# Two graph layers on one core: weight bursts of seven pairs, a seventh pair in the spare accumulator bank, and two numerators moved

## The chip, the cores and the metric

The kernel runs on one core of a Trainium2 chip. The metric is the device time of one execution in microseconds (us). The engines are named as in the profile: PE is TensorE's matmul, PEld its weight load, DVE is VectorE, ACT is ScalarE, POOL is GpSimd, SP is SyncE, which here only issues transfers. All data are float32, some of it in the reduced form float32r[...].

## The reference

There are B = 8 batches, N = 2048 nodes and C = 64 features. `A` is the row-normalised adjacency matrix. Both layers add a graph convolution to x and normalise:

```python
def layer0(x, A, embedding, weight, bias):        # K = 3
    As = [I, A, 2 * A @ A - I]
    w = einsum('nd,dkio->nkio', embedding, weight)      # a weight matrix for each node
    x_g = einsum('knm,bmc->bnkc', stack(As), x)
    return einsum('bnki,nkio->bno', x_g, w) + embedding @ bias

def layer1(x, E, A, weights_pool, bias_pool):
    supports = [I, A, 2 * A @ A - I, softmax(relu(E @ E.T), axis=1)]
    # the same three einsums with four supports

x = layernorm(x + layer0(x, adj, ...))
x = layernorm(x + layer1(x, E, adj, ...))
```

The node embeddings have D = 16 elements. Three kinds of work follow from this: products of an adjacency block with x or with `u = A x` (called *products* here), the making of the *weights* w of each node from its embedding, and the *apply*, which multiplies each node's features by its own weights.

## The kernel before

**Stages.** The nodes are cut into 8 blocks of 256. There are five phases of 8 stages, one per block j: A0 (stages 0 to 7, u = A x of layer 0), B0 (8 to 15, A u), A1 (16 to 23), Z1 (24 to 31, the softmax support) and V1 (32 to 39). Most stages form their product by Strassen's scheme: seven products p1 .. p7 in the order `usual = (1, 4, 7, 2, 6, 5, 3)` (other orders for the first and the last stage of V1). Each product has 8 steps, so such a stage has a length of 56 steps. DVE and ACT read a product's accumulator when it is done and combine the parts: p1 and p4 are copied by ACT, the others are added by DVE.

**The plan.** Everything that isn't a product is written into a plan by hand: `put(n, place, job)` puts a job into stage n at a place between 0 and 64, which is scaled to the stage's length (place x 56/64 steps). While PE goes through the products of stage n, each job is issued after the first step that reaches its place. All instructions are pinned, so on every engine the order of the program is the order of execution[...].

**Weights.** `Stage.weights` (L327) makes w for the 256 nodes of a block. A *pair* here is two matmuls of 64 rows each (h = 0 and h = 1), one on the upper and one on the lower half of TensorE's rows[...]. Their stationary operand is a part of a chunk `wst` (8 pairs; 512 KB, loaded by SP), the moving one is `e2`, the block's embeddings. Two pairs fill one buffer `pw`: two PSUM banks, one for each half. Then ACT or DVE copies the buffer into `w_room`, the only room for w. A full stage has 32 pairs in 16 groups of two. They are made in bursts of three groups (`cuts = (0, 3, 6, 9, 12, 14, 16)`), since the pool `ps_big` has three buffers of two banks. They go round in turn among all users: `pw`, the apply's `po`, the turn's `pt`, scores `ps`, row scores `pr`, bias `pb`. V1 begins with one group alone at place 4. The stages of A0, B0 and A1 have their weights made in the following stage, those of V1 in their own.

**Accumulators.** The other two banks are `ps_acc`, one bank each, used in turn by the products: while one is filled, the other is read.

**Other jobs that the text speaks of.** `apply` (L348) fills four `po` buffers, one after the other, and DVE takes each in by four SCALAR_TENSOR_TENSOR. In V1 the four applies of the previous stage stand at place 4, ahead of the weights at the same place. `turn` (L414) transposes u or x through a buffer `pt`; half of it is copied to `t` by ACT, half by DVE. In A1 the turn of u stands at place 4 of the next stage. `statistics` (L722) runs two exponentials on ACT, at place 62 of an A1 stage (for j = 0 at 19 of the next). `Sums.make` (L746) forms the right-hand sums of Strassen's scheme on DVE. `numerators` (L676) makes exponentials of scores for the softmax support; in stage 24 they serve stage 25, which is called narrow, at places 3, 5, 7 and 10, with two `normalize` at 37 and 40.

**Weight loads.** `Ahead` (L228) keeps up to three chunks: `next` first fills, that is it issues the load of the next chunk into the room that came free, and then hands out the oldest.

## Time and profile before

| what | value |
|---|---|
| time, median of 3 runs (lowest to highest) | 1467.65 us (1466.69 to 1468.63) |
| the profiled execution | 1470.19 us, of which the span is 1468.3 us |
| granted TensorE clock | 0.998 |
| PE MATMUL of the weights, pw | 1728, 297 ns each by the profile, 146.5 us busy |
| ACT copies w <- pw, 128x1024 | 330, 1021 ns each |
| DVE copies w <- pw, 128x1024 | 118, 1224 ns each |
| DVE evacuation of the applies, acc <- po | 640, 426 ns each |
| DMA wst <- wd, 512 KB, SP | 108, 6.1 us from issue to landing |

Durations of matmuls overlap[...]. So the cost of a stretch of PE's work is read from the starts, by taking the distance from the first start to the start of what follows.

In the timeline each line has the start, the time until the last of its instructions ends, the engine, the source line (all have L43, since a helper issues them), the operation, the tiles written and read, the shape and the count; in brackets the idle time before and what ended it. In the list of waits a line has who waited, what for, the total in us, how many times, and the longest.

### The profile page before, as it was taken

Reading aid. Unit: us, or ns where it says so; the run is one execution under the profiler, and the core shown is the slowest. Engines: PE = TensorE matmul, PEld = TensorE weight load, DVE = VectorE, ACT = ScalarE, POOL = GpSimd, SP = SyncE. Lnnn points to the kernel's source line nnn. Section 1 sums busy time; section 2 is a strip of 40 time slices with the busy share of each in tenths; the row PEclk is TensorE's granted clock in tenths of the full one; section 3 lists DMA queues with packets and bytes.
Section 4 is the critical chain, followed back from the end, with each engine's and each line's share of the span. In section 5 each row is a group of like instructions: output and inputs, shape, how many; then the busy total and the mean of one; then the engine's idle time right before and its main releaser. Section 6 shows DMA issues by size and latency. Waiting matters only on the chain.

```text
span 1468.3 us, 31599 instructions
## 1 busy us (share of the span) xinstructions
PE 1440.8 (98%) x13502; PEld 1184.9 (81%) x13502; DVE 973.9 (66%) x1655; ACT 478.3 (33%) x597; POOL 204.6 (14%) x339
## 2 busy tenths in 40 slices
PE   9999999999999999999999999999999999999996
PEld 4577777778999999567777777799888988888885
DVE  3866666648676766865666666679794666666666
ACT  0444444432211213154444344612110233333332
POOL 4212221110111111211011111011000000000000
PEclk9999999999999999999999999999999999999999
DMA  9888888886666666578887977223313766666662
GB/s 361 274 262 276 282 280 265 281 313 190 209 192 201 205 201 206 157 177 180 205 201 162 207 205 186 35 73 101 90 44 105 236 196 190 189 194 191 190 206 59
DMA packets 88380, 285.50 MB, mean 194 GB/s; under 512 B 14000, under 2 KB 19632, under 8 KB 86640
## 3 DMA queue, kind: packets, MB, share of 16 engines
q1 hardware_dynamic: 55568, 175.13, 41.0%
q0 software_dynamic: 27200, 94.71, 21.4%
q10 hardware_dynamic: 5472, 13.63, 2.8%
q8 instruction: 107, 1.75, 0.5%
q14 instruction: 33, 0.27, 0.1%
HBM read 217.33 MB, written 62.41 MB: 191 GB/s over the span
## 4 chain that ended last, share of the span: by engine, by line
PE 91%; DVE 4%; DMA 3%; ACT 1%; issue 1%; ACTq 0%; DVEq 0%
PE p L43 58%; PE po L43 14%; PE pw L43 9%; PE pu L43 4%; PE pz L43 4%; DMA wst<-wd 2%; PE pt L43 1%; PE pr L43 1%; PE ps L43 1%; DVE acc L43 1%; DMA x<-in_x 1%; DVE u L43 1%; DVE t L43 0%; DVE p L43 0%; ACT t L43 0%
## 5 line engine op out<-in xcount | busy, mean ns | idle before, releaser
L43 ACT ACTIVATE w<-pw 128x1024 f32<-128x1024 f32 x330 | 320.1, 1021 | 444.4 <-PE pw L43 442.6
L43 DVE SCALAR_TENSOR_TENSOR acc<-po,mask,acc 128x256 f32<-128x256 f32 (+1 forms) x640 | 247.1, 426 | 66.8 <-PE po L43 56.5
L43 DVE COPY w<-pw 128x1024 f32<-128x1024 f32 x118 | 144.4, 1224 | 142.3 <-PE pw L43 142.1
L43 PE MATMUL p<-a,u 128*128 128x128 f32 x1920 | 234.1, 278 | 0.6 <-issue 0.6
L43 PEld LDWEIGHTS p<-a,u 128*128 128x128 f32 x1920 | 221.2, 192 | 8.8 <-issue 2.4
L43 PE MATMUL po<-w,t 128*32 128x256 f32 (+1 forms) x5120 | 206.9, 337 | 7.0 <-issue 5.8
L43 PE MATMUL p<-u,a 128*128 128x256 f32 x832 | 204.3, 388 | 0.0
L43 PEld LDWEIGHTS po<-w,t 128*32 128x32 f32 (+1 forms) x5120 | 128.3, 108 | 79.3 <-issue 16.3
L43 PEld LDWEIGHTS p<-u,a 128*128 128x128 f32 x832 | 151.6, 190 | 29.2 <-issue 5.4
L43 PE MATMUL p<-x,a 128*128 128x256 f32 x624 | 152.4, 384 | 0.0
L43 PE MATMUL pw<-e,wst 64*128 64x256 f32 x1728 | 146.5, 297 | 4.3 <-DMA wst<-wd 2.5
L43 PEld LDWEIGHTS pw<-e,wst 64*128 64x128 f32 x1728 | 112.5, 184 | 46.0 <-issue 23.9
L43 PEld LDWEIGHTS p<-x,a 128*128 128x128 f32 x624 | 114.7, 190 | 19.3 <-issue 0.5
L43 PE MATMUL p<-a,x 128*128 128x128 f32 x768 | 93.0, 277 | 0.0
L43 PEld LDWEIGHTS p<-a,x 128*128 128x128 f32 x768 | 88.3, 192 | 2.5 <-PE pw L43 0.2
L43 PE MATMUL pu<-x,a 128*128 128x512 f32 x192 | 87.0, 600 | 2.1 <-DMA x<-in_x 2.1
L43 PE MATMUL p<-w,u 128*128 128x256 f32 x384 | 85.8, 379 | 0.0
L43 PE MATMUL p<-a,w 128*128 128x128 f32 x672 | 81.3, 277 | 0.0
L43 PEld LDWEIGHTS p<-w,u 128*128 128x128 f32 x384 | 72.0, 190 | 9.3
L43 PEld LDWEIGHTS p<-a,w 128*128 128x128 f32 x672 | 77.3, 192 | 2.5 <-issue 1.4
L43 PEld LDWEIGHTS pu<-x,a 128*128 128x128 f32 x192 | 35.1, 190 | 42.7 <-issue 37.1
L43 DVE TENSOR_TENSOR temps<-p,temps 128x256 f32<-128x256 f32 x115 | 45.8, 420 | 34.1 <-PE p L43 33.3
(129 smaller groups left out, 1372.7 us busy)
## 6 DMA issues: line engine op xcount, KB each, us to landing
wst<-wd SPq DMA_DIRECT2D x108, 512.0 KB, 6.1
a<-in_adj_q SPq DMA_DIRECT2D x90, 512.0 KB, 5.3
a<-sd SPq DMA_DIRECT2D x88, 512.0 KB, 4.6
sd<-a POOLq DMA_DIRECT2D x24, 512.0 KB, 6.3
bx<-bx POOLq DMA_DIRECT2D x32, 256.0 KB, 5.9
acc<-bx POOLq DMA_DIRECT2D x16, 512.0 KB, 7.1
pd<-acc POOLq DMA_DIRECT2D x16, 512.0 KB, 5.3
acc<-pd POOLq DMA_DIRECT2D x16, 512.0 KB, 8.7
```

What stands on the lines that cost most here:

```text
L43: return self._tc.keep_in_program_order(f(*args, **kwargs))
```

## The change

The weights are now cut in pairs, not in groups. In 21 stages (the weights of A0 with j = 1 to 6, of A1 with j = 0 to 6, and of all of V1) the cuts are 0, 4, 11, 18, 25, 32: one burst of four pairs and four of seven. Six of the seven fill the three buffers of two banks; the seventh goes into the accumulator bank that no product is using. As that is one bank for both halves[...]: the h = 0 half is issued first in the burst and the h = 1 half last, the others are shifted by one against each other, and the last one waits for a read of one element by ACT from the first one's result. The other stages keep their bursts. The accumulator pool is written as two tags of one buffer, so that the spare one can be named. The copies are dealt anew: one group in each burst goes to DVE (with exceptions in A0 and V1), the single seventh pair is copied by ACT, second in order. Chunks are loaded at the end of a burst instead of at the start of the next. The places of the bursts change with their number, in A0 the turn, the apply and the post that follow move by 1 to 1.5 places, and the numerators of the narrow stage are set further apart.

```diff
-    ps_acc = ctx.enter_context(tc.tile_pool(name="ps_acc", bufs=2, space=PSUM))
+    ps_acc = ctx.enter_context(tc.tile_pool(name="ps_acc", bufs=1, space=PSUM))
...
+    in_use = [0]
+    in_turn = mybir.DependencyInfo(mybir.DependencyClass.Sync, mybir.DependencyReason.DATA)
+
+    def acc_bank(i):
+
+        return ps_acc.tile([P, BC], F32, tag=f"acc{in_use[0] ^ i}", name="pa")
...
-        def next(self):
-            self.fill()
+        def next(self, fill=True):
+            if fill or not self.ready:
+                self.fill()
             return self.ready.pop(0)
...
+        def weights(self, v0, v1):
+            if v0 == 0:
                 self.w = w_room[:, 0:NB * self.units].rearrange("p (n o) -> p n o", n=NB)
...
+                self.ws = {}
+            for c in range(v0 // 8, (v1 - 1) // 8 + 1):
+                if c not in self.ws:
+                    self.ws[c] = wst.next(fill=False)
+            pairs = list(range(v0, v1))
+            made = [(v, big("pw").rearrange("p h (v n) -> p h v n", n=NB)) for v in pairs[:-1:2]]
+            spare = []
+            if len(pairs) % 2:
+                spare = [pairs.pop()]
+                made.append((spare[0], acc_bank(1).rearrange("p (h v n) -> p h v n", h=2, n=NB)))
+            for at in zip(spare + pairs, pairs + spare):
+                for h, v in enumerate(at):
+                    r = slice(64 * h, 64 * h + 64)
+                    i, ps = (v - v0) % 2, made[(v - v0) // 2][1]
+                    ins = pe.matmul(ps[:, h, i, :], self.ws[v // 8][r, v % 8, :], self.e2[r, :], start=True, stop=True)
+
+                    if v in spare and not h:
+                        seen = act.activation(small.tile([1, 1], F32, tag="seen", name="seen"), ps[0:1, h, i, 0:1], AF.Copy)
+                    elif v in spare:
+                        tc.add_manual_dep(ins.ins, seen.ins.name, in_turn, reason="one bank, two row tiles")
+            wst.held = 1 if v1 % 8 else 0
+            wst.fill()
+            if spare:
+                made.insert(1, made.pop())
+            for k, (v, ps) in enumerate(made):
+                m = 1 if v in spare else 2
+                dst = self.w[:, :, 2 * v:2 * v + 2 * m].rearrange("p n (v h) -> p n v h", h=2)
+                on_dve = k == len(made) // 2 and v not in spare and self.n and (v > 16 if self.phase == "A0" else self.phase != "V1" or v0)
+                copy(0 if on_dve else 1, dst, ps.rearrange("p h v n -> p n v h"))
...
         def accumulator(self, name):
-            return ps_acc.tile([P, BC], F32, tag="acc", name=name)
+            in_use[0] ^= 1
+            return acc_bank(0)
...
-        cuts = (0, 3, 6, 9, 12, 14, 16) if st.units == C else (0, 3, 6, 8)
-        if phase == "V1" and st.j:
-            put(n, 4, st.weights, 0, 1)
-            cuts = (1, 4, 7, 10, 13, 16)
+
+        sevens = phase == "V1" or n in (*range(1, 7), *range(16, 23))
+        cuts = (0, 6, 12, 16) if st.half else (0, 4, 11, 18, 25, 32) if sevens else (0, 6, 12, 18, 24, 28, 32)
         weights = [(st.weights, *g) for g in zip(cuts, cuts[1:])]
+
+        def place_weights(n, places):
+            for place, job in zip(places, weights):
+                put(n, place, *job)
...
-            spread(n + 1, 1, 31, weights)
-            turned, bursts, posts = 33, (38, 38, 38, 38), (50,)
+            if sevens:
+                place_weights(n + 1, (1, 5, 14, 23, 32))
+                turned, bursts, posts = 34.5, (39.5, 39.5, 39.5, 39.5), (51,)
+            else:
+                spread(n + 1, 1, 31, weights)
+                turned, bursts, posts = 33, (38, 38, 38, 38), (50,)
...
-            spread(n + 1, 12, 34.5, weights)
+            if sevens:
+                place_weights(n + 1, (1, 6, 14, 23.2, 32.3))
+            else:
+                spread(n + 1, 12, 34.5, weights)
             turned, bursts, posts = 4, (43, 43, 43, 43), (56,)
...
-            spread(n, (22 if 0 < st.j < 7 else 12 if st.j else 4), (62 if st.j < 7 else 42), weights)
+            place_weights(n, (4, *((14, 23.2, 32.3, 41.5) if st.j in (0, 7) else (23.2, 32.3, 41.5, 50.7))))
...
-            for t, places in enumerate(((3, 5, 37), (7, 10, 40))):
+            for t, places in enumerate(((3, 7, 22), (37, 39.5, 57))):
```

More of the change, by code (lines that the diff above doesn't have):

```diff
@@ L324, in bias @@
                 pool.dma_start(out=rows, in_=heads(bx))
-        def weights(self, g0, g1):
-            if g0 == 0:
+        def weights(self, v0, v1):
+            if v0 == 0:
                 self.w = w_room[:, 0:NB * self.units].rearrange("p (n o) -> p n o", n=NB)
-            made = []
-            for g in range(g0, g1):
-                if g % 4 == 0:
-                    self.ws = wst.next()
-                ps = big("pw").rearrange("p h (v n) -> p h v n", n=NB)
-                for i in range(2):
-                    for h in range(2):
-                        r = slice(64 * h, 64 * h + 64)
-                        pe.matmul(ps[:, h, i, :], self.ws[r, 2 * (g % 4) + i, :], self.e2[r, :],
-                                  start=True, stop=True)
-                made.append(ps)
-            if g1 == self.units // 4:
-                wst.fill()
-            for g, ps in zip(range(g0, g1), made):
-                dst = self.w[:, :, 4 * g:4 * g + 4].rearrange("p n (v h) -> p n v h", h=2)
-                copy(0 if self.n and g % (8 if self.phase == "A0" else 3) == (2 if self.phase == "A0" else 1) else 1, dst, ps.rearrange("p h v n -> p n v h"))
+                self.ws = {}
[26 more added lines that the diff above has]
+                copy(0 if on_dve else 1, dst, ps.rearrange("p h v n -> p n v h"))
```

## The prediction

> **What bounds the kernel now.** I read the page first (busy shares, chain of waits, groups), then the timeline of TensorE (PE) in one V1 stage, then the same for VectorE (DVE) and ScalarE (ACT) at the two places where the change puts new work, then the list of waits of PE.

> ```profile
> PE 1440.8 (98%) x13502; PEld 1184.9 (81%) x13502; DVE 973.9 (66%) x1655; ACT 478.3 (33%) x597; POOL 204.6 (14%) x339
> ...
> PE 91%; DVE 4%; DMA 3%; ACT 1%; issue 1%; ACTq 0%; DVEq 0%
> ...
> L43 ACT ACTIVATE w<-pw 128x1024 f32<-128x1024 f32 x330 | 320.1, 1021 | 444.4 <-PE pw L43 442.6
> ```

> PE sets the end: it is busy 98% of the span and makes 91% of the chain. So every microsecond taken from PE's stream counts, and every wait put into it counts too. ACT is idle two thirds of the time, and its largest work is copying the weights.

> ```profile
> 1228.89 0.51 PE L43 MATMUL pw<-e,wst 64*128 64x256 f32 x4
> 1229.32 2.27 PE L43 MATMUL p<-a,u 128*128 128x128 f32 x18
> 1231.44 5.30 PE L43 MATMUL p<-a,x 128*128 128x128 f32 x46
> 1236.67 0.98 PE L43 MATMUL pw<-e,wst 64*128 64x256 f32 x12
> 1237.57 2.27 PE L43 MATMUL p<-a,x 128*128 128x128 f32 x18
> ```

> Starts count here (ends overlap). A burst of 2 pairs takes 0.43 us up to the next product matmul, one of 6 pairs 0.90: so (0.90 - 0.43)/4 = 0.118 per pair and 0.195 fixed. 46 product matmuls in 5.23 are 0.112 each, less the last, which stands 0.205 before the burst (0.093 too much); 18 right after a burst take 2.11 instead of 2.01. Each burst costs 0.195 + 0.093 + 0.10 = **0.39 to 0.40 us beside its pairs**.

> ```profile
> 1223.85 7.90 DVE L43 SCALAR_TENSOR_TENSOR acc<-po,mask,acc 128x256 f32<-128x256 f32 x16 [2.60 <-PE po L43]
> ```

> This is DVE evacuating the four po buffers that precede the burst at 1228.89: 0.494 us each, so the third buffer is free at 1223.85 + 12 x 0.494 = 1229.8, after that burst began.

> ```profile
> 753.23 1.15 ACT L43 ACTIVATE sq<-sq,low 128x1024 f32<-128x1024 f32 x1 [3.85 <-DVE low L43]
> ...
> 754.38 1.14 ACT L43 ACTIVATE row<-row,low 128x1024 f32<-128x1024 f32 x1
> 755.42 0.19 ACT L43 ACTIVATION_READ_ACCUMULATOR row<-row,low 128x1 f32 x1
> 755.63 1.26 ACT L43 ACTIVATE t<-pt 64x512 f32<-64x512 f32 x2
> ```
> ```profile
> 756.92 1.40 DVE L43 COPY t<-pt 64x512 f32<-64x512 f32 x2 [3.45 <-ACT t L43]
> ```

> This is the start of stage 20 (A1, j = 4; it begins at 752.53). ACT runs two exponentials until 755.61, then half of the turn's copies; DVE's half waits for ACT's and ends at 758.3. The burst at 758.24 takes that buffer last, and just gets it.

> ```profile
> PE pw L43 <- DMA wst<-wd: 2.5, 4, 0.8
> ...
> PE ps L43 <- DVE t L43: 1.3, 1, 1.3
> ...
> PE pw L43 <- DVE p L43: 0.7, 1, 0.7
> ```

> PE's few waits: late weight chunks in A1, and two waits in stage 24, where numerators crowd the turn.

> [...]The trace's plain copies agree in the slope (375 ns for 256 columns, 1021 for 1024: 0.84 ns), but leave 0.16 us for the fixed part.[...]

> **The change, part by part.** Own time of the profiled execution: 1470.19 us, its span 1468.3; the median is 1467.65, 2.5 less. I sum differences and add them to the median.

> 1. *Fewer bursts.* Twenty-one stages (weights of A0 j = 1..6, A1 j = 0..6, all of V1) go from six bursts to five with the same 32 pairs: 21 x 0.40 = **-8.4**.

> 2. *The small read*, 4 per such stage, 84 in all. The ordered product is the last of the burst; its weight load is due 0.224 + 5 x 0.113 - 0.11 = 0.68 us after the burst's start (intervals of single matmuls at 1236.67 and after). The first pair ends at 0.39 (389 ns is the longest pw matmul), ACT starts 0.08 after a pw group's end, the read takes 0.16 to 0.18, and PE resumes 0.05 after ACT's end (ACT's u ends at 626.94, PE's transposes start at 626.99): 0.69. So it is late by some 0.04. Bounds: nothing, if the read is quicker[...]. I take 0.04: 84 x 0.04 = **+3.4** (0 to 12.6). ACT stands free at nearly all bursts: in A0 with all copies on ACT (0.92 us apart for a big one, about 0.5 for the small one, then a 0.39 temps copy) it is done 4.3 us after a burst, and the next comes after 4.7. In stage 2 a DMA issue on ACT waits for the sums' store until 81.0: **+0.5** once. The spare's copy comes second and ends 2.2 to 2.3 us after the burst's start, the next product wants the bank after 2.5 to 2.7: covered.

> 3. *V1, first burst now four pairs.* The buffers go round by three: x, y, z, x for the four applies, then y, z for the burst's two groups. Before, only y was used. Now the second group needs z, the third apply's, free at 1229.8; its weight load is due at 1228.89 + 0.34 - 0.11 = 1229.12 and starts at 1229.84, and four pairs that took 0.67 (168.82 to 169.49) take 1.38. +0.71 in seven stages (j = 1..7): **+5.0**. ACT and DVE have time to spare at the other V1 bursts (p6's adds of 1.6 us fit in the 2.0 before the next burst).

> 4. *V1, j = 0.* The spare bank of the burst at place 23.2 is that of p2, whose adds stand in DVE behind three sums of 2.29 us and a weight copy: two sums from 1152.1 to 1159.0 (the old copy between them is gone), the copy to 1160.2, the third sum to 1162.4, the adds to 1163.2. The burst comes 20.5 steps of 0.446, one burst of four pairs and one of seven after 1150.49, at 1161.7: **+1.5**. The last burst moves from 62 to 41.5, and the po wait of 0.4 at 1183.7 goes: **-0.4**.

> 5. *A1, bursts at 1 and 6 around the turn at 4.* In stage 20's times: the first burst starts at 753.05 and delays the turn by 0.67 + 0.20 to 755.12..755.99; the next burst starts at 756.95. ACT: exponentials to 755.61, then the first group's copy (queued ahead of the turn's) to 756.64, the turn's two to 757.9; DVE's two follow, to 759.3. The seven-pair burst takes three buffers, and its third is the one of the transposes: due 757.4, free 759.37. **+2.0 us** in each of six stages (18 to 23; the exponentials lie alike in all six): +11.8. In stage 17 the exponentials are earlier but u's copy ends at 626.94: its burst waits 1.4, while the old 1.0 before the turn shrinks to 0.2: +0.5. Together **+12.3**.

> 6. *Weight loads.* The fill now follows the burst; in A1 chunk 3 is issued near 758 and wanted near 767.9, 9.9 us later; in the three stages with a real wait the load took 8.6 to 8.7 and was wanted some 0.8 sooner. The waits of 2.5 go: **-2.5**. SP's queue holds the adjacency loads behind each weight load as before.

> 7. *Numerators of stage 25 in stage 24.* At 3, 7 and 37, 39.5 they no longer claim the turn's buffer: the waits of 1.34 and 0.75 go, with some 0.2 of restarts: **-2.3**. The normalisations (2.3 us of DVE each) lie beside the products; first use is in stage 25.

> 8. Other bursts keep their sizes; who copies which group shifts by one or two, at no cost while PE has 2.8 us or more between them.

> Sum: -8.4 + 3.4 + 0.5 + 5.0 + 1.5 - 0.4 + 12.3 - 2.5 - 2.3 = **+9.1**. 1467.65 + 9.1 = 1476.8 (1479.3 for a profiled execution).

> **Rivals.**
> - *Faster: the A1 wait isn't there.* One mechanism: whether the turn's buffer is free when the seven-pair burst of A1 asks for it (part 5). If ACT serves the turn in time, 11.8 + 1.4 drop out: 9.1 - 13.2 = -4.1, **1463.5**. It decides from 0.6 us per stage instead of 2.0 (9.1 - 6 x 1.4 = 0.7). For it: the old burst got the same buffer without a wait. Against: it did so by some 0.2 us only (free at 758.31, its weight load due near 758.6), and both the earlier place and the extra ACT copy go the wrong way.
> - *The read is dear.* At 0.15 late each, 84 x 0.15 = 12.6 instead of 3.4: +18.3, **1486**. For it: it is in line 84 times[...]. Against: the 0.16 us from this trace.
> - *A balance.* The A1 wait half as long and the read hidden: 9.1 - 5.9 - 3.4 = about 0, **1467.5**.

> **How the numbers follow.** Forecast 0.62, its own range 1471 to 1483 (read 0 to 0.1, A1 wait 1.5 to 2.2); faster 0.22; dear read 0.08; balance 0.08. A difference of 0.2% (2.9 us) is about what this measurement can tell from none. Slower 0.62 + 0.08 = 0.70, same 0.08, faster 0.22. The range from 1460 to 1484 leaves out the lower part of the faster case and the dear read.

> **What would show it.** Of the changed profile: one burst fewer in each of 21 stages; in A1 a gap of about 2 us inside the burst of 14, ended by DVE t; in V1 one of 0.6 inside the first burst, ended by DVE acc; no waits of pw for wst; none of ps for DVE t in stage 24. ACT seen with 0.16 to 0.3 us each. I am wrong if the A1 bursts run through in 1.0 us, or if the last pair stands more than 0.1 behind in bursts with a free ACT.

## The result, and the profile after

| kernel | time, median (lowest to highest) | against before |
|---|---|---|
| before | 1468.14 us (1466.69 to 1469.04), 4 runs | |
| after | 1490.59 us (1489.48 to 1495.47), 4 runs | ratio 1.016, 95% interval 1.0135 to 1.0185 |

The changed kernel is slower by 22.4 us. The forecast was slower, too, but by 9.1 us: the direction held, the size did not. The profiled executions are 1470.19 (before) and 1489.48 us (after), their spans 1468.3 and 1487.7: 19.4 us apart. The granted TensorE clock fell from 0.998 to 0.994.

The page of the kernel after shows busy shares, the chain that ended last, and the groups of the weights:

```profile
PE 1443.0 (97%) x13502; PEld 1189.5 (80%) x13502; DVE 968.0 (65%) x1649; ACT 504.1 (34%) x729; POOL 204.5 (14%) x339
...
PE 85%; DVE 8%; ACT 2%; DMA 2%; issue 1%; ACTq 0%; SPq 0%; DVEq 0%
...
L43 ACT ACTIVATE w<-pw 128x1024 f32<-128x1024 f32 x294 | 301.2, 1046 | 300.1 <-PE pw L43 296.6
...
L43 PE MATMUL pw<-e,wst 64*128 64x256 f32 x1560 | 143.0, 291 | 16.9 <-DVE t L43 11.4
```

PE has the same 13502 matmuls and is busy for 2.2 us more, but in the chain PE fell from 91% to 85% and DVE rose from 4% to 8%: PE now waits for DVE. The weight matmuls alone stood idle 16.9 us, 11.4 of it until DVE's `t` was done. The list of waits says the same (who waited for what, total us, times, longest):

```profile
PE pw L43 <- DVE t L43: 11.4, 7, 1.7
...
PE pw L43 <- DVE acc L43: 3.8, 7, 0.5
PE pa L43 <- DMA wst<-wd: 1.7, 1, 1.7
PE pw L43 <- DVE p L43: 1.7, 2, 1.0
PE pa L43 <- ACT seen L43: 1.3, 3, 0.6
PE pa L43 <- ACT temps L43: 1.3, 1, 1.3
```

The first two rows are the predicted waits, in place and number: the turn's buffer in A1 and the third `po` buffer in V1. The third is a weight chunk that comes late (1.7 us; before, four waits made 2.5). In the fourth, one wait of 0.7 is the one of before, which the new places were to remove, and one of 1.0 is new. The read's row is three waits, of which the prediction foresaw the one in stage 2, and the last row was not foreseen. These six rows are 21.2 us. The three rows shown of before (2.5, 1.3 and 0.7) made 4.5, and 8.4 us should be gained by fewer bursts: 21.2 - 4.5 - 8.4 = 8.3, but the span grew by 19.4. Some of what is missing is waits that the list puts under "issue", as it names no releaser for them; among them is the one of 1.5 us that part 4 predicted for V1, j = 0. But something also costs time that isn't a wait. The timeline of PE in stage 20 shows it:

```profile
760.01 1.03 PE L43 MATMUL pa<-x,a 128*128 128x256 f32 x4
760.97 0.38 PE L43 MATMUL pa<-e,wst 64*128 64x256 f32 x1
760.97 0.85 PE L43 MATMUL pw<-e,wst 64*128 64x256 f32 x8
763.51 0.51 PE L43 MATMUL pw<-e,wst 64*128 64x256 f32 x4 [1.70 <-DVE t L43]
763.82 0.27 PE L43 MATMUL pa<-e,wst 64*128 64x256 f32 x1
764.02 1.98 PE L43 MATMUL pa<-x,a 128*128 128x256 f32 x4
765.80 3.20 PE L43 MATMUL pa<-u,a 128*128 128x256 f32 x10
```

ACT and DVE in the same stage show why the buffer is late:

```profile
759.64 1.02 ACT L43 ACTIVATE w<-pw 128x1024 f32<-128x1024 f32 x1
760.69 1.25 ACT L43 ACTIVATE t<-pt 64x512 f32<-64x512 f32 x2
761.97 0.16 ACT L43 ACTIVATE seen<-pa 1x1 f32<-1x1 f32 x1
```
```profile
761.98 1.39 DVE L43 COPY t<-pt 64x512 f32<-64x512 f32 x2 [2.90 <-ACT t L43]
```

ACT copies the first burst's group, then its half of the turn, then DVE does the other half until 763.37; the last pairs start at 763.51. This is the queue that the prediction's part 5 went through.

The trace also records each stretch at a reduced grant. Both kernels have one at the very end (from 1461.8 us before, from 1480.9 after). Up to there the kernel before has none; the kernel after has three, each 3.41 us long at 0.5, from 764.1, 808.5 and 897.3. Each follows one of the six waits of 1.70 us in A1. A stage of A1 with one of them is 44.7 us long, one without 43.05 (stage 18 has 44.86, as it has the late chunk).

Cut at the starts of the applies, the 19.4 us lie as follows:

| stretch | after less before, us |
|---|---|
| to the end of stage 2's wait for the read | +0.6 |
| A0, the six stages with five bursts | -0.49 each |
| B0 (bursts and places as before) | +1.25 |
| stage 17 | +0.28 |
| A1, stages 18 to 23 | +3.17, +1.67, +2.61, +2.42, +1.66, +2.48: +14.0 |
| stage 24, with the numerators | +0.39 |
| Z1 and V1, j = 0 | +1.13 |
| V1, j = 1 to 6 | +0.40 to +0.44 each: +2.5 |
| V1, j = 7 | +2.18 |

### The profile page after: what moved, and what is told of

It reads as the page before. It is cut to its first block, busy times and chain, and to the rows that moved or that the text cites. A ratio compares the mean times of both kernels' runs of the same rounds, so it can differ in the third digit from the quotient of the medians.

```text
span 1487.7 us, 31626 instructions
## 1 busy us (share of the span) xinstructions
PE 1443.0 (97%) x13502; PEld 1189.5 (80%) x13502; DVE 968.0 (65%) x1649; ACT 504.1 (34%) x729; POOL 204.5 (14%) x339
## 4 chain that ended last, share of the span: by engine, by line
PE 85%; DVE 8%; ACT 2%; DMA 2%; issue 1%; ACTq 0%; SPq 0%; DVEq 0%
PE pa L43 65%; PE po L43 11%; PE pw L43 6%; DVE acc L43 4%; PE pt L43 1%; PE ps L43 1%; PE pr L43 1%; DVE t L43 1%; DMA x<-in_x 1%; DMA wst<-wd 1%; ACT sq L43 1%; ACT t L43 1%; DVE row L43 1%; DVE u L43 1%; ACT row L43 1%
## 5 line engine op out<-in xcount | busy, mean ns | idle before, releaser
L43 ACT ACTIVATE w<-pw 128x1024 f32<-128x1024 f32 x294 | 301.2, 1046 | 300.1 <-PE pw L43 296.6
L43 DVE SCALAR_TENSOR_TENSOR acc<-po,mask,acc 128x256 f32<-128x256 f32 (+1 forms) x640 | 247.1, 427 | 67.2 <-PE po L43 56.8
L43 PE MATMUL pa<-a,u 128*128 128x128 f32 (+1 forms) x2048 | 262.3, 284 | 2.7 <-issue 2.7
L43 PEld LDWEIGHTS pa<-a,u 128*128 128x128 f32 x2048 | 244.5, 192 | 14.3 <-issue 5.2
L43 DVE COPY w<-pw 128x1024 f32<-128x1024 f32 x112 | 137.2, 1225 | 173.2 <-PE pw L43 172.6
L43 PE MATMUL pa<-x,a 128*128 128x256 f32 (+1 forms) x816 | 243.9, 440 | 0.7 <-DMA x<-in_x 0.7
L43 PE MATMUL po<-w,t 128*32 128x256 f32 (+1 forms) x5120 | 206.4, 337 | 6.0 <-issue 4.9
L43 PE MATMUL pa<-u,a 128*128 128x256 f32 x832 | 202.3, 390 | 0.0
L43 PEld LDWEIGHTS pa<-x,a 128*128 128x128 f32 x816 | 150.4, 191 | 62.3 <-issue 38.6
L43 PEld LDWEIGHTS po<-w,t 128*32 128x32 f32 (+1 forms) x5120 | 129.1, 108 | 77.3 <-issue 13.4
L43 PEld LDWEIGHTS pa<-u,a 128*128 128x128 f32 x832 | 154.6, 193 | 30.1 <-issue 5.3
L43 PE MATMUL pw<-e,wst 64*128 64x256 f32 x1560 | 143.0, 291 | 16.9 <-DVE t L43 11.4
L43 PEld LDWEIGHTS pw<-e,wst 64*128 64x128 f32 x1560 | 111.2, 184 | 34.1 <-ACT w L43 13.9
L43 PE MATMUL pa<-a,x 128*128 128x128 f32 x768 | 92.9, 277 | 0.0
L43 PEld LDWEIGHTS pa<-a,x 128*128 128x128 f32 x768 | 88.3, 192 | 2.3
L43 PE MATMUL pa<-w,u 128*128 128x256 f32 x384 | 85.8, 379 | 0.0
L43 PE MATMUL pa<-a,w 128*128 128x128 f32 x672 | 81.3, 277 | 0.0
L43 PEld LDWEIGHTS pa<-w,u 128*128 128x128 f32 x384 | 72.0, 190 | 9.3
L43 PEld LDWEIGHTS pa<-a,w 128*128 128x128 f32 x672 | 77.3, 192 | 2.5 <-issue 1.4
L43 DVE TENSOR_TENSOR t<-pa,temps 64x256 f32<-64x256 f32 x128 | 53.7, 419 | 30.8 <-PE pa L43 29.8
L43 DVE TENSOR_TENSOR temps<-pa,temps 128x256 f32<-128x256 f32 x115 | 45.9, 420 | 32.7 <-PE pa L43 32.1
L43 ACT ACTIVATE sq<-acc 128x1024 f32<-128x1024 f32 (+2 forms) x19 | 17.5, 922 | 139.9 <-DVE acc L43 139.9
```

The source lines that it names most:

```text
L43: return self._tc.keep_in_program_order(f(*args, **kwargs))
```

## The experiments

All runs stand beside runs of the kernel before on the same chip (medians 1466.6 to 1467.8). Differences of two experiments are differences of their ratios, times 1467. By the intervals of the table they are good to about 3 us, and to about 4.5 us where the changed kernel (1.016) is one of the two.

| kernel | median, us | ratio to before, 95% interval |
|---|---|---|
| A1 in six bursts | 1473.66 | 1.0046, 1.0028 to 1.0064 |
| A1 alone in five | 1489.9 | 1.015, 1.0129 to 1.0171 |
| A1's first burst copied by DVE | 1481.78 | 1.0099, 1.0082 to 1.0117 |
| A1, a copy twice | 1498.52 | 1.0209, 1.0194 to 1.0224 |
| six, V1's first burst later | 1466.74 | 1.0002, 0.9994 to 1.001 |
| six, old numerators | 1472.52 | 1.0043, 1.003 to 1.0055 |
| six, V1's ends as before | 1469.5 | 1.002, 1.0013 to 1.0027 |
| joined | 1464.92 | 0.9989, 0.9982 to 0.9995 |
| joined, A1's five bursts later | 1510.52 | 1.0294, 1.0277 to 1.0311 |

### Where the time is: A1 with and without the change

First A1 alone was put back to bursts of three groups:

```diff
-        sevens = phase == "V1" or n in (*range(1, 7), *range(16, 23))
+        sevens = phase == "V1" or n in range(1, 7)
```

> The changed kernel with the A1 weights back in six bursts from place 12 on; all else as changed. Theory (the loss sits in A1: a wait of 1.9 us for the turn's buffer in each of seven stages, and in some of them TensorE at half its clock for 3.4 us after it, 1.7 us each): A1 gained 14 us in the trace of the change, so the time falls by 14 to 17, to about 1475, and no stretch at half clock is left in A1. Rival (the prediction's own sizes; the rest of the loss is spread over other stages): it falls by 8, to about 1482.

It took 1473.66 us: (1.016 - 1.0046) x 1467 = 16.7 us of the 22.4 belong to the seven stages' bursts of A1. No stretch at half clock is left in A1 in its profile (granted clock 0.998, as before). Then the reverse, the change in A1 alone, with the old bursts in A0 and V1 and the old numerators:

```diff
-        sevens = phase == "V1" or n in (*range(1, 7), *range(16, 23))
...
+        sevens = n in (16, 17, 18, 19, 20, 21, 22)
...
-            for t, places in enumerate(((3, 7, 22), (37, 39.5, 57))):
+            for t, places in enumerate(((3, 5, 37), (7, 10, 40))):
```

> Only the A1 weights in bursts of four and seven pairs at 1, 6, 14, 23.2 and 32.3; A0, V1 and the numerators as before. Theory: A1 alone costs 14 to 17 us, so 1482 to 1485 beside 1468. Rival: 8 us, 1476.

1489.9 us, +22: even more than theory expected. The wait is the same, 1.97 from start to start in six stages; four of the six are followed by 3.41 us at half clock (granted clock of this execution 0.993). PE also stands still within one apply and just after another (2.9 and 1.6 us from start to start), where neither before nor after has a pause; the profile names no releaser for either, so their cause is open.

### The wait made shorter and longer

In the next two kernels, only the queue ahead of the turn's copies changes. In the first, DVE copies both groups of A1's first burst, so that ACT is free for the turn; in the second, ACT copies the first group twice.

```diff
                 on_dve = k == len(made) // 2 and v not in spare and self.n and (...)
+                on_dve = on_dve or self.phase == "A1" and v1 == 4
```
```diff
                 copy(0 if on_dve else 1, dst, ps.rearrange("p h v n -> p n v h"))
+                if self.phase == "A1" and v1 == 4 and not k:
+                    copy(1, dst, ps.rearrange("p h v n -> p n v h"))
```

> The changed kernel, but in A1 both groups of the first burst are copied by DVE, so that no ACT copy stands ahead of the turn's. Theory: DVE's turn copies end 1.0 us sooner, the wait of 1.97 between two pw matmuls becomes about 1.0, and TensorE isn't slowed after so short a wait: 7 x 0.95 + 3 to 4 x 1.7 = 12 to 13 less, about 1478. Rival (the half clock comes from something else, such as more 64-row matmuls early in the stage): 6.6 less, about 1484, with the stretches at half clock still there.

> The changed kernel, but in A1 ACT copies the first group twice (the same values again), so that the turn's copies come 0.9 us later still. Theory: the wait grows to about 2.9 us and TensorE is slowed after it in nearly all seven stages: 7 x 0.9 + 3 to 4 more stretches x 1.7 = 11 to 13 more, about 1502. Rival (half clock not tied to the wait): 6.5 more, about 1497, with about three stretches as before.

With DVE the time fell by (1.016 - 1.0099) x 1467 = 8.9 us. The list of waits of this kernel, and its PE timeline in stage 20:

```profile
PE pw L43 <- DVE t L43: 8.5, 7, 1.2
```
```profile
758.74 0.85 PE L43 MATMUL pw<-e,wst 64*128 64x256 f32 x8
760.81 0.50 PE L43 MATMUL pw<-e,wst 64*128 64x256 f32 x4 [1.22 <-DVE t L43]
761.12 0.27 PE L43 MATMUL pa<-e,wst 64*128 64x256 f32 x1
761.32 1.13 PE L43 MATMUL pa<-x,a 128*128 128x256 f32 x4
```

In six stages the wait is shorter by 0.48 us, not by the 1.0 expected: the burst delays the turn itself, so ACT's copies can't start when ACT becomes free. In stage 17 it was 1.21 already and stays so. 6 x 0.48 is 2.9 us (11.4 - 8.5), and yet 8.9 went. Most of the rest is the clock: there is no stretch at half clock any more (granted clock 0.998), and the four matmuls at 761.32 take 1.13, not 1.98.

With the double copy the wait grew by 0.16 only, not by the 0.9 expected (2.13 from start to start; ACT's second copy now ends last), but the time by (1.0209 - 1.016) x 1467 = 7.2 us. With 1498.5 us the time is nearer to the rival's 1497 than to theory's 1502, but the rival's three stretches did not come. Here four of the six waits, and two pauses in stage 17, are followed by half clock, seven stretches of 3.41 us in all against three (granted clock 0.990 against 0.994). At some 1.7 us each, half of 3.41, that is 6.8 more. One of the two pauses is the shorter wait for the turn, now 1.58 us; the other, 2.6 us within an apply, has no named releaser and doesn't exist in the kernel after, so the copy isn't all that differs in the profile. In both kernels, the small change of the wait explains less than half, and the number of half-clock stretches most of the rest.

### What brings the half clock

To see the price by itself, pauses of seven lengths (`sizes`) were made where there was no stretch at half clock, in the B0 stages 9 to 15 of the joined kernel (below), three in each stage:

```diff
+    def dose(n, columns):
+        t = one.tile([P, NB], F32R, tag="dose", name="dose")
+        ps = big("pd")
+        pe.matmul(ps[:, 0, 0:NB], stages[n].e2[:, 0:P], stages[n].e2, start=True, stop=True)
+        for m in columns:
+            act.activation(t[:, 0:m], ps[:, 0, 0:m], AF.Copy)
+        pe.matmul(ps[:, 1, 0:NB], stages[n].e2[:, 0:P], t, start=True, stop=True)
...
+    for n in range(9, 16):
+        for k, place in enumerate((34, 45, 56)):
+            put(n, place, dose, n, sizes[(n + 2 * k) % 7])
```

> A measurement of the half clock by itself. The joined kernel, with 21 made waits in the B0 stages 9 to 15 (three in each, at places 34, 45 and 56): a matmul, two to five ACT copies of 128 or 256 columns that read it, and a matmul that reads the copy; nothing of their results is used. Start to start the two matmuls should lie 1.2 to 2.3 us apart, in seven sizes. Theory (a pause of PE alone brings the half clock, by its length): none of the 1.2 and 1.4, at most one of the three 1.55, about half of those from 1.77 up, nearly all of 2.3; each slowed one costs 1.7, so the time is that of the joined kernel (1464.9) plus some 37 for the waits plus some 10 to 17, with stretches of 3.41 us at 0.5. Rival (the half clock belongs to A1's mix of short-row bursts, transposes and waits, or comes by chance): no stretch at 0.5 in stages 9 to 15, about 1502.

> The same 21 made waits at places 37, 48 and 60, so that they fall at other times. Expected as in the first of the two.

They took 1536.3 and 1540.5 us (one run each), at granted clocks of 0.986 and 0.982. Half clock did come in B0 (0.50 from 458.56 in the first), so it doesn't belong to A1's mix. But the expected rates by the length of the wait were wrong: of the eight pauses of 2.03 to 2.15 us from start to start only one was followed by it. By these counts the length alone doesn't decide. Many pauses also grew to 3 or 4 us because other work stood in ACT's queue; of the twelve of 3 us and more, eleven were followed.

To see what sets the followed waits apart, the trace of the kernel after can be cut into stretches of 3.413 us, as long as those at half clock. Their three starts there (764.1, 808.5, 897.3) are 13 and 26 such lengths apart, so one of them fixes all cuts. The six waits of A1 in stages 18 to 23, each with the stretch that follows (each row: the stretch, its length, then busy us of PE, PEld, DVE, ACT and POOL, granted clock, DMA share and GB/s):

```profile
671.99:675.40 3.41, 1.92 (x16) 1.33 (x14) 1.32 (x2) 3.07 (x5) 0.00 (x0) 1.00 1.64 180
675.40:678.81 3.41, 3.21 (x17) 2.79 (x18) 1.28 (x2) 1.78 (x3) 0.00 (x0) 1.00 1.01 47
716.36:719.77 3.41, 2.41 (x20) 1.82 (x18) 0.83 (x2) 3.33 (x7) 0.00 (x0) 1.00 0.74 88
719.77:723.18 3.41, 2.71 (x15) 2.37 (x16) 1.78 (x2) 1.99 (x4) 0.00 (x0) 1.00 0.72 36
760.73:764.15 3.42, 1.72 (x17) 1.19 (x16) 2.13 (x3) 2.29 (x5) 0.00 (x0) 1.00 1.37 40
764.15:767.56 3.41, 3.41 (x9) 2.66 (x10) 0.47 (x1) 1.86 (x3) 0.00 (x0) 0.50 0.67 34
805.11:808.52 3.41, 1.71 (x17) 1.18 (x16) 1.77 (x3) 2.59 (x5) 0.00 (x0) 1.00 0.79 39
808.52:811.93 3.41, 3.41 (x12) 2.65 (x10) 0.84 (x1) 1.89 (x3) 0.00 (x0) 0.50 0.61 37
849.48:852.90 3.42, 1.74 (x14) 1.17 (x14) 1.48 (x3) 2.89 (x5) 0.00 (x0) 1.00 1.55 68
852.90:856.31 3.41, 3.39 (x18) 2.96 (x19) 1.13 (x1) 1.78 (x3) 0.00 (x0) 1.00 0.77 38
893.85:897.27 3.42, 1.72 (x16) 1.32 (x13) 2.60 (x3) 2.29 (x5) 0.00 (x0) 1.00 0.70 34
897.27:900.68 3.41, 3.41 (x10) 2.70 (x9) 0.00 (x0) 1.10 (x2) 0.00 (x0) 0.50 0.53 48
```

The wait is 1.69 or 1.70 us in all six. In stages 20, 21 and 23 it lies wholly in one stretch, whose PE is busy 1.71 or 1.72 of 3.41 us, and the next stretch has 9 to 12 matmuls at a clock of 0.50. In stage 22 the last 0.02 us of the wait fall over the cut, PE is busy 1.74, and the clock stays at 1.00. In stages 18 and 19 the cut lies 0.20 and 0.70 us before the wait's end, PE is busy 1.92 and 2.41, and the clock stays, too. Two of the made pauses, one of each kind:

```profile
410.78:414.19 3.41, 1.74 (x17) 1.54 (x15) 2.77 (x11) 1.43 (x4) 0.00 (x0) 1.00 0.02 5
414.19:417.60 3.41, 3.41 (x30) 3.41 (x31) 2.06 (x4) 0.00 (x0) 0.00 (x0) 1.00 0.28 91
455.15:458.56 3.41, 1.61 (x12) 1.42 (x13) 0.80 (x4) 1.53 (x4) 0.00 (x0) 1.00 0.02 5
458.56:461.97 3.41, 3.41 (x19) 3.41 (x18) 1.64 (x3) 0.00 (x0) 0.00 (x0) 0.50 0.24 36
```

PE busy 1.74: the next stretch has 30 matmuls at full clock. PE busy 1.61: 19 at half.

So in these eight pairs PE was busy for 1.61 to 1.72 us where half clock followed and for 1.74 and more where it did not. That this share decides is the author's estimate from these rows and was not shown: 0.02 us lie between the two kinds, and the ends of matmuls are modelled. Whether anything besides the matmuls counts stays open.

### The smaller terms

The remaining kernels are built on the one with A1 in six bursts. V1's first burst two or three steps later:

```diff
-            place_weights(n, (4, *(...)))
+            place_weights(n, (4 if not st.j else 6.6, *(...)))
```

> As the kernel with A1 in six bursts (1473.7 us beside a before of 1467.0), and V1's first burst of four pairs stands at place 6.6 instead of 4 in j = 1 to 7, that is two or three product steps after the applies. Theory (the burst's second group waits 0.71 us for the po buffer that DVE has not emptied): the wait goes in seven stages, -5.0, about 1468.7, and no PE pw <- DVE acc is left. Rival (the buffers and engines are only as fast as before, so the wait comes back at the next burst or at a product): 1473.7.

1466.74 us, ratio 1.0002: (1.0046 - 1.0002) x 1467 = 6.4 less, or 6.0 against the twin with the old numerators. The row "PE pw <- DVE acc" is gone from the list of waits. The numerators at their old places:

```diff
-            for t, places in enumerate(((3, 7, 22), (37, 39.5, 57))):
+            for t, places in enumerate(((3, 5, 37), (7, 10, 40))):
```

> As the kernel with A1 in six bursts (1473.7 us), with the numerators of stage 24 at their old places. Prediction's step (the new places take two waits of 1.34 and 0.75 away): 2.3 us slower, 1476.0. Theory now (the new places only move the waits, 2.2 us of them are in the trace of after as well): 1473.7, within 0.7.

1472.52 us, ratio 1.0043 against 1.0046: no difference to be seen. The two intervals together leave some 3 us of room, so these times alone don't exclude the 2.3 us. The lists of waits show that little could come of the move: at the old places PE waits 1.3 us for DVE's `t` and 0.8 for DVE's `p`, at the new ones 0.7 and, newly, 1.0. In the kernel after, DVE and then PE near the end of stage 24:

```profile
952.01 2.35 DVE L43 TENSOR_TENSOR p<-p,c 128x1024 f32<-128x1024 f32 x2
...
954.55 0.67 DVE L43 SCALAR_TENSOR_TENSOR p<-ps,c 128x512 f32<-128x512 f32 x1
```
```profile
955.27 0.51 PE L43 MATMUL pw<-e,wst 64*128 64x256 f32 x4 [0.96 <-DVE p L43]
```

The normalisation, now at 22, is 2.35 us of DVE ahead of the read that frees the score's buffer, and a weight burst waits for that buffer. The two ends of V1 with their old bursts:

```diff
-        sevens = phase == "V1" or n in (*range(1, 7), *range(16, 23))
...
+        sevens = n in (1, 2, 3, 4, 5, 6, 33, 34, 35, 36, 37, 38)
...
+                if st.j:
+                    put(n, 4, st.weights, 0, 2)
+                spread(n, (22 if 0 < st.j < 7 else 12 if st.j else 4), (62 if st.j < 7 else 42), weights)
```

> As the kernel with A1 in six bursts (1473.7 us), and the first and the last V1 stage have their old bursts of three groups. Theory (the spare bank of these two stages belongs to a product whose reader is held up, 1.55 us at j = 0 and 1.3 + 0.45 at j = 7; their segments are 1.13 and 2.18 us longer than before): -3.3, about 1470.4. Prediction's step (only j = 0 waits, its po wait falls by as much as is won): within 0.8 of 1473.7.

1469.5 us: (1.0046 - 1.002) x 1467 = 3.8 less, beside 3.3 expected. The kernel after shows what was missed in the last stage (ACT, DVE, then PE):

```profile
1447.47 1.06 ACT L43 ACTIVATE sq<-acc 128x1024 f32<-128x1024 f32 x1 [1.66 <-DVE acc L43]
1448.43 0.35 ACT L43 COPY temps<-pa 128x256 f32<-128x256 f32 x1
```
```profile
1443.61 1.23 DVE L43 COPY w<-pw 128x1024 f32<-128x1024 f32 x1 [3.74 <-PE pw L43]
1444.76 1.21 DVE L43 TENSOR_REDUCE mean<-acc 128x16 f32<-128x1024 f32 x1
...
1446.21 1.22 DVE L43 TENSOR_TENSOR acc<-acc,mean 128x1024 f32<-128x1024 f32 x1
```
```profile
1448.84 0.39 PE L43 MATMUL pa<-e,wst 64*128 64x256 f32 x1 [1.26 <-ACT temps L43]
```

The spare bank belongs to p4 until ACT has copied it. That copy stands in ACT's queue behind a square, the square waits for DVE's mean, and the mean waits behind a weight copy. So the next burst, which begins with the spare bank, waits at its first matmul.

### A version that keeps what paid

Bursts of seven for A0, j = 2 to 6, and V1, j = 1 to 6, alone; V1's first burst at 6.6 in these; the old bursts in A1 and at V1's ends; the old numerators:

```diff
-        sevens = phase == "V1" or n in (*range(1, 7), *range(16, 23))
...
+        sevens = n in (2, 3, 4, 5, 6, 33, 34, 35, 36, 37, 38)
...
```

> What is left of the change where it paid: bursts of seven pairs for the weights of A0 j = 2 to 6 and of V1 j = 1 to 6 alone, V1's first burst at place 6.6 in these, A1 and V1's two ends in the old bursts, the numerators at their old places. Theory: 1473.7 less 3.3 (ends of V1), less 0.7 x 6 (first burst), less 0.8 (stage 2) = about 1465.4, some 1.5 below before's 1467.0. Rival (a five-burst stage gives its 0.4 back by later transfers and the copies' new order): 1467 to 1469.

1464.92 us, ratio 0.9989 (0.9982 to 0.9995): faster than both kernels, and by what was expected, 1.6 us. One more attempt moved A1's five bursts to where the turn's buffer is free, with the apply and the post later:

```diff
-                place_weights(n + 1, (1, 6, 14, 23.2, 32.3))
+                place_weights(n + 1, (6, 14, 23.2, 32.3, 41.5))
...
-            turned, bursts, posts = 4, (43, 43, 43, 43), (56,)
+            turned, bursts, posts = 4, (47.5,) * 4 if sevens else (43,) * 4, (58.5,) if sevens else (56,)
```

> The joined kernel with five bursts in A1 as well, at 6, 14, 23.2, 32.3 and 41.5 (the first, of four pairs, after the turn and with the two buffers that the turn doesn't use; the first seven-pair burst where the old kernel got the turn's buffer in time), the apply at 47.5 and the post at 58.5 in place of 43 and 56. Theory (only the turn's buffer made the A1 wait): no wait of 1.97 and no half clock, 7 x 0.4 = 2.8 less than the joined kernel's ratio of 0.9989, that is 0.997. Rival (the last burst collides with the scores at 38 and 40, the apply with those at 57 and 60): waits of about 1 us in each stage, ratio 1.001 to 1.004.

1510.52 us. This version also computes wrong values: in stage 23 its last burst reads the embeddings of stage 24, since their load at place 37 precedes it, so part of one block's weights is another's, and PE waits 6.6 us for the load. The row of the turn is gone, but the last burst has another wait:

```profile
PE pa L43 <- ACT seen L43: 14.7, 7, 2.4
...
PE pw L43 <- DVE row L43: 3.3, 6, 0.5
```

The small read now stands behind the two exponentials on ACT (839.16 to 841.43 in one stage). In six stages the last matmul of the burst waits 2.3 to 2.4 us for it, and each of these six waits is followed by half clock, for 3.41 or 6.83 us (granted clock of the profiled execution 0.984). The rival was right, and too cheap: 0.0305 x 1467 = 45 us more than the joined kernel, 6.6 of which are the load. For five bursts in A1 a place with no such collision was not found.

## Why the prediction was right in sign and wrong in size

It said 1476.8 us and a range up to 1484; the kernel took 1490.6. By its own steps, for the profiled execution:

1. *Fewer bursts, -0.40 each*: right. In A0, where neither kernel has a listed wait of PE from stage 3 on, a stage gained 0.49.
2. *The small read, +3.4*: wrong, it is nearly free. The tile's own view in the kernel after (number, shortest, median and longest duration in ns; then who waited for it):

```profile
L43 ACT ACTIVATE seen<-pa x84: 143/160/162, 81.5 to 1459.6; 1x1 f32<-1x1 f32 x84
...
  PEld pa L43: 1.9, 3
  PE pa L43: 1.3, 3
```

 Three of the 84 held PE, for 1.3 us in all. The duration of 0.16 was taken well. (The 0.15 of the dear read stands for a read of some 0.3 us. In the trace before, ACT's smallest ACTIVATE, `dev<-dev,eps` of 128x4, does take 297 ns, but it reads a second operand, and this read has none.) But the first pair ends earlier in the burst than was assumed: in the median reads end 0.638 us after the burst's start, with the weight load due at 0.68 to 0.70. Stage 2's wait of 0.6 came as predicted (0.5). The kernel without the read was not run, so what the order itself is worth was not shown.
3. *V1's first burst, +5.0*: right; 0.82 from start to start, some 0.71 more than without a wait, in seven stages, and 6.0 to 6.4 us when it is taken away.
4. *V1, j = 0, +1.5 - 0.4*: the wait came (1.55), the `po` wait stayed (0.58). The same mechanism in the last stage, +2.18, was not looked for: its chain goes from PE over ACT and DVE to a weight copy.
5. *The turn's buffer in A1, +12.3*: this is the term that failed in size. Cause, place and length were right: six waits of 1.86 us (1.97 less the usual 0.11) for 2.0. What failed is the step from a wait to its cost: the prediction took a wait of 2.0 us as 2.0 us. The traces show about 1.7 us more for each wait that is followed by 3.41 us at a clock of 0.50. The A1 stages 18 to 23 came out at +14.0; by parts 1, 2, 5 and 6 they should have at 11.8 - 2.4 + 1.0 - 2.5 = +7.9. The difference is 6.1: three stretches at half clock are some 5.1, a late weight chunk is 1.7 (part 6), the free read and the slightly shorter wait take off 1.0 and 0.6, and some 0.9 is not accounted for.
6. *Weight loads, -2.5*: the four waits went, but one of 1.7 came (at 685.81).
7. *Numerators, -2.3*: wrong. The wait of 1.34 went, but the one of 0.75 stayed (0.71) and one of 0.96 came. It asked where the two waits go, and not what is late next: +0.39 in the trace, no difference to be seen in the experiment.
8. *The rest at nothing*: B0 is 1.25 longer in the profiled execution. Its bursts keep their sizes and places, but its copies are dealt anew and its chunks are loaded at the end of a burst. By the records PE stands idle there for 6.6 us instead of 5.5, nearly all of it in and just after the applies, where the profile names no releaser. The cause is open.

From +9.1 to +19.4: A1 +6.1, numerators +2.7, last stage of V1 +1.7, B0 +1.25, V1's start +0.3, A0 -1.4, V1's middle -0.3. The median is 3 us further off than the profiled execution. The runs of the kernel after spread over 6.0 us, those of before over 2.4. The granted clocks of its four runs fall as their times rise: 0.994, 0.993, 0.990 and 0.989 for 1489.48, 1489.68, 1491.5 and 1495.47 us. By an estimate from the lengths (1.7 us of 1490 is 0.0011), 0.005 less is some four stretches at half clock more, about 7 us. Only the first of the four has a trace, so those of the others can't be counted.

Of the rivals, the faster one fell: the turn's buffer was late as computed. The dear read, 1486, came nearest in time, for a wrong reason: that is luck. The sign isn't, since the wait that brings most of the loss was foreseen; but the read, charged with 3.4 us and nearly free, hid a part of what was missing elsewhere. No rival held that a wait could cost more than its length.

## What to carry to other kernels

A larger burst over a rotating pool pays only where every buffer it takes is free by then: go through the queue of each reader (here ACT's copy ahead of the turn, a square ahead of the accumulator's copy), stage by stage, first and last stages too, and keep the change where none is late; half of this one gave 0.11%, all of it cost 1.6%. In a kernel like this one, where PE is the bound, a wait can cost more than its length: of six waits of 1.70 us of idle PE three were followed by 3.41 us at a clock of 0.50 here, and four in the kernel with A1 alone, at some 1.7 us more each; with 1.22 us none was. Where a change brings waits of such a length, price them with and without this, and look at the granted clock after each in the trace. If a job is moved away from a wait, look for what it stands ahead of at its new place.

## What had not been expected of the hardware

In the kernel after, 3.41 us at a clock of 0.50 followed three of six waits of 1.69 to 1.70 us, so the same wait cost 1.9 us in one stage and, by an estimate from the two lengths, 3.6 in another (stages of 43.05 and 44.7 us). A wait shortened from 1.70 to 1.22 of idle time in six stages thus gave 8.9 us in place of 2.9. On the other hand the order of the seventh pair's two matmuls by way of ACT (a one-element read of 160 ns) held PE at 3 of 84 bursts only, with six other pairs in between (74 of the reads ended within 0.65 us of the burst's start); in the last kernel, behind two exponentials, the same read held PE for 2.3 us.
